# A four-layer graph network with two mixtures of experts: first tiles of the second mixture from the rows routed so far, and five reordered seams

## The chip, the cores and the metric

The kernel runs on one core of a Trainium2 chip. The metric is the device time of one execution in microseconds (us); the median of three runs stands for a kernel. One further execution was profiled, and the views quoted here come from it. The engines are TensorE (PE, its weight loads as PEld), VectorE (DVE), ScalarE (ACT), GpSimd (POOL) and SyncE (SP), which issues most of the transfers. Each engine works through its own list of instructions in order.

## The reference, cut to what matters

A graph of 2,708 nodes with 256 features each goes through four layers. Each is a graph convolution and then a feed-forward block, both with a layer norm in front and a residual. The change lies in layers 1 to 3:

```python
x = x + L1_gnn(layernorm(x), adj)        # graph attention, 4 heads of 64
x = x + L1_ffn(layernorm(x))             # first mixture: H = gelu(x @ W1 + b1), 1024 wide
    # assign = argmax(softmax(H @ Wg + bg)); y = H @ Wd[assign] + bd[assign]; out = prob * y
x = x + L2_gnn(layernorm(x), adj)        # graph attention, 1 head of 256
x = x + L2_ffn(layernorm(x)):            # decoder block
    # x = x + causal_attention(rmsnorm(x)) @ wo.T    4 heads, 2 shared keys and values
    # probs = softmax(rmsnorm(x) @ router.T); the two largest of 8, weights divided by their sum
    # out += weight[e] * ((silu(h @ w1[e].T) * (h @ w3[e].T)) @ w2[e].T)     682 wide
x = x + L3_gnn(layernorm(x), adj)        # graph attention, 1 head, elu
x = x + linear(layernorm(x))
```

## The kernel before

The nodes lie in 22 row tiles of 128 (the last has 20 rows) and in 6 blocks of 512 (the last has 148). `X` holds the features in SBUF throughout. A framework tracks tiles and buffers and places each engine's instructions in order by its own estimates, within the dependences; `tc.issue_after(i)` forbids an instruction of the same engine to be placed before `i`. A tile of a pool with `bufs=n` is reused after n others, when their last reader is done.

**`gat_heads`** (layer 1) takes two heads at a time, `p` = 0 and 1. For each of the 22 source tiles `j` the attention weights `e` are made, multiplied with `V` into six accumulators `acc` (L780) and with `low` into the denominators `den` (L788). After the last `j`, `den` is copied to `ds`, transposed, inverted to `rd`; then each of six accumulators is copied to `o`, transposed, multiplied by `rd` into `y` (L822) and added to `X` (L829).

**`top1_ffn`** (first mixture) takes layer-norm statistics (`ln_stats`: sums on DVE in groups of four tiles, a root on ACT, L147), then block after block: `features` (normalise, transpose), `hidden` (32 records of PE, L911, Gelu on ACT), `gate` (logits, first maximum, rank of each row in its expert, and its number scattered to `fnodes` in DRAM), and `store`, which transposes hidden rows and writes them to DRAM (`hr` L926, three buffers). The last two blocks are stored after the last gate. `route.finish` then turns the counts into a list of tiles: each expert owns one tile for certain, the others follow, 26 in all as a rule. The node numbers of each tile are loaded from `fnodes` (L1550, L1554) as a column, 128 pieces of 4 bytes per tile, converted (L980), and used to gather hidden rows (`fetch`, L990). Each tile is transposed (L1003), multiplied with the expert's `wd`, and scattered to DRAM.

**`decoder_ffn`** (layer 2). In `attention`, each of six blocks is attended over all source tiles up to it (scores L1736, exponents L1749, values L1755); sums of exponents go by DVE and, for every third `j`, by POOL (L1761), and end in `pd` (L1767). The generator `send` runs a block behind, beside the next block's attention: projection `wy`, residual, root-mean-square norm, router logits `pr`, then `route.chunk` (first and second choice, rank L1423, scatter of normalised rows `h` to `hs` in DRAM, L1444). `yield` is where attention goes on; `steps` sets the pace. The last block's `send` runs alone after attention, then `route.finish`.

**`experts`** runs 47 tiles as a rule. Tiles 0 to 7 are the first 128 rows of experts 0 to 7. A step of its loop holds: `fetch` (rows `f` from `hs`, L1543 or L1550, five buffers), `front` (transposes, L116, copy `ft` L1891), `hidden` (w1 and w3, L1909), `silu` (L1922), `gate` (L1926), `transposes` (`pt` L1933), `results` (`po` L1941, copy `y`, indirect scatter `send` L1573) and `place` (`route.where`, L1563 to L1567: the rows of `ys` that the tile's results go to, held in `to`, eight buffers). After the first tiles' gate come `shares` (softmax of the routing logits) and `Head` (weights of layer 3). `route.others` guards tiles beyond the usual number.

**The join.** `Routing.combine` loads both results of each row from `ys` in six blocks (L1594) over SP and ACT and adds them to `X` (L1604) block after block, with layer 3's statistics between. `reload_graph` brings the mask back from DRAM, and `mark_empty` (L2084, L2085) writes a row of it on ACT's queue.

Of the kernel before, what the change touches and what calls it, by code (L numbers as in the profile page):

```python
# [16 lines left out]
P = 128  # L17
# [660 lines left out]
def gat_heads(net):  # L678
# [8 lines left out]
    Q = len(cols) // 2  # L687
    with ExitStack() as ctx:
        big = ctx.enter_context(tc.tile_pool(name="g1big", bufs=1))
        V = big.tile([P, NT, H, DH], F32, name="V")  # L690
        ratio = big.tile([P, NT, H], F32, name="ratio")

        low = big.tile([P, NT, H, 2 * Q - 1], F32, name="low")
        big_p = big.tile([P, H, N], F32, name="big_p")
# [73 lines left out]
        for p in range(2):  # L768
# [3 lines left out]
            nc.tensor.matmul(den, zero, big_p[0:1, 0, :512], start=True, stop=False, skip_group_check=True)  # L772
            for j in range(NT):
                e = wide.tile([P, 2, N], F32, name="e")
                for k, h in enumerate(heads):
                    gat_pairs(net, e[:, k, :], j, 0, N, big_p[:, h, :], ratio[:, j, h : h + 1])
                for n, (i0, iw) in enumerate(cols):
                    for k, h in enumerate(heads):
                        half = slice(k * DH, (k + 1) * DH)
                        nc.tensor.matmul(  # L780
                            acc[n][half, :iw], V[:, j, h, :], e[:, k, i0 : i0 + iw], start=j == 0, stop=j == NT - 1
                        )
                for q in range(Q):
                    for k, h in enumerate(heads):
                        for half in range(2):
                            i0, iw = cols[half * Q + q]
                            g = (2 * k + half) * 32
                            nc.tensor.matmul(  # L788
# [6 lines left out]
                            )  # L795

            ds = small.tile([P, 512], F32, name="ds", bufs=1)
# [4 lines left out]
            rd = small.tile([P, 4, 4, Q], F32, name="rd", bufs=1)  # L802
# [4 lines left out]
            out = []  # L807
            for n, (i0, iw) in enumerate(cols):
                o = small.tile([P, 512], F32, name="o", bufs=3)
                (nc.vector.tensor_copy if n % 2 else nc.scalar.copy)(o[:, :iw], acc[n][:, :iw])  # L810
                pt = paux.tile([P, 4, P], F32, name="aux")
                its = tiles_of(i0, iw)
                for c, i in enumerate(its):
                    r = rows(i)
                    nc.tensor.transpose(pt[:r, c, :], o[:, c * P : c * P + r], net.ident)
                whole = [c for c, i in enumerate(its) if rows(i) == P]
                for c0, c1, r in [(0, len(whole), P)] + [(c, c + 1, rows(its[c])) for c in range(len(whole), len(its))]:
                    nt = c1 - c0
                    y = small.tile([P, 4, 2, DH], F32, name="y")

                    d = rd.rearrange("p c (k b) q -> p c k b q", b=2)[:r, c0:c1, :, n // Q, n % Q]
                    nc.vector.tensor_tensor(  # L822
                        y[:r, :nt],
                        pt[:r, c0:c1, :].rearrange("p c (k d) -> p c k d", d=DH),
                        d.unsqueeze(3).to_broadcast([r, nt, 2, DH]),
                        ALU.mult,
                    )
                    xs = X[:r, its[0] + c0 : its[0] + c1, p * 2 * DH : (p + 1) * 2 * DH]
                    nc.vector.tensor_tensor(xs, xs, y[:r, :nt].rearrange("p c k d -> p c (k d)"), ALU.add)  # L829
# [27 lines left out]
def top1_ffn(net, ctx):  # L857

    nc, tc, a, X = net.nc, net.tc, net.a, net.X
    E, HID = 8, 1024
    KC = HID // P
    with ExitStack() as inner:
        big = ctx.enter_context(tc.tile_pool(name="f1big", bufs=1))
        dram = ctx.enter_context(tc.tile_pool(name="f1dram", bufs=1, space=bass.MemoryType.DRAM))
        wd = inner.enter_context(tc.tile_pool(name="f1wd", bufs=1, side="right")).tile([P, E, KC, D], F32, name="wd")
# [11 lines left out]
        for e in range(E):  # L879
            nc.sync.dma_start(wd[:, e], a["f1_wd"][e].rearrange("(c p) m -> p c m", p=P))  # L880
        route = Routing(net, big, dram, 1, "f")
        ln = net.ln_stats()
# [3 lines left out]
        with tc.tile_pool(name="f1tp", bufs=2, space=PSUM) as ptp, tc.tile_pool(  # L886
# [7 lines left out]
            def features(its):  # L894
                ft = work.tile([P, 2, 512], F32, name="ft")
                for k, t in enumerate(its):
                    r = rows(t)
                    f = rp.tile([P, D], F32, name="f", bufs=2)
                    net.normed(f, t, ln)
                    ps = net.transposed(ptp, f, r)  # L900
                    nc.vector.tensor_copy(ft[:, :, k * P : k * P + r], ps[:, :, :r])
                return ft

# [14 lines left out]
            def store(its, halves):  # L918

                for k, t in enumerate(its):  # L920
                    r = rows(t)
                    for n, half in enumerate(halves):
                        hr = rp.tile([P, 512], F32, name="hr", bufs=3)
# [3 lines left out]
                        (nc.scalar.copy if n else nc.vector.tensor_copy)(  # L927
                            hr[:r], ps[:r].rearrange("p c m -> p (c m)")
                        )
                        nc.sync.dma_start(rows_of[span(t), n * 512 : (n + 1) * 512], hr[:r])  # L930
# [17 lines left out]

            blocks, kept = chunks(512), []
            ft = features(tiles_of(*blocks[0]))  # L950
            for n, (n0, nw) in enumerate(blocks):
                its = tiles_of(n0, nw)
                halves = hidden(ft, nw)
                if n + 1 < len(blocks):
                    ft = features(tiles_of(*blocks[n + 1]))
                gate(its, halves, nw)
                kept.append((its, halves))
                if n + 2 != len(blocks):
                    for k in kept:
                        store(*k)  # L960
                    kept.clear()
        route.finish()
        prep = ctx.enter_context(tc.tile_pool(name="g2prep", bufs=1))
        with tc.tile_pool(name="f1t", bufs=1, space=PSUM) as pt, tc.tile_pool(
# [3 lines left out]
            nc.scalar.dma_start(bd.rearrange("p e d -> p (e d)"), a["f1_bd"].rearrange("e d -> (e d)").partition_broadcast(P))  # L968

            node, number, to = (  # L970
                sp.tile([P, route.tiles], t, name=name, bufs=1)
                for t, name in ((F32, "node"), (I32, "number"), (I32, "to"))
            )
            usual = route.usual
            groups = [range(E)] + [range(s, min(s + 4, usual)) for s in range(E, usual, 4)]
            held = {}

            def numbers(group):
                g = slice(group[0], group[-1] + 1)
                nc.vector.tensor_copy(number[:, g], node[:, g])  # L980

            def places(group):
                g = slice(group[0], group[-1] + 1)
                at = sp.tile([P, E], F32, name="at", bufs=2)[:, : len(group)]
                nc.vector.tensor_tensor(at, node[:, g], route.taken[:, g], ALU.mult)
                nc.vector.tensor_tensor(to[:, g], at, route.spare[:, g], ALU.add)

            def fetch(s):
                hr = held[s] = sp.tile([P, 2, 4, P], F32, name="hr", bufs=5)
                nc.gpsimd.indirect_dma_start(  # L990
# [22 lines left out]
            route.load_first(node[:, :E])  # L1013
            for s in range(E, usual):
                route.load(s, node[:, s : s + 1])
            numbers(groups[0])
            for s in range(4):
                fetch(s)
            ready = transposes(0)
            route.owners()  # L1020
            places(groups[0])
# [3 lines left out]
            def through(s0, s1, ready):  # L1025
                last = added = None
                for s in range(s0, s1):
# [14 lines left out]
                    route.send(to[:, s : s + 1], y)  # L1042
                    with tc.issue_after(added.ins):
                        for g in groups[1:]:
                            if s + 6 == g[0]:
                                numbers(g)
                                places(g)
                        if s == 3:
                            heads.append(Head(net, prep, one, "g2", True, nc.scalar))
# [4 lines left out]
            with route.others():  # L1054
                group = range(usual, route.tiles)
                for s in group:
                    route.load(s, node[:, s : s + 1])
                numbers(group)
                places(group)
# [32 lines left out]
def gat_single(net, key, head, feed, elu):  # L1092
# [7 lines left out]
    with ExitStack() as ctx:  # L1100
# [6 lines left out]
        nc.gpsimd.memset(V[:, LAST], 0.0)  # L1107
# [1082 lines left out]
```

## Time and profile before

| what | value |
|---|---|
| time, median of 3 runs | 2879.4 us (2875.14 to 2881.12) |
| the profiled execution | 2876.56 us |
| its span | 2874.8 us |
| mean granted TensorE clock | 0.951 of full speed |
| PE busy | 2630.7 us, 92% |
| DVE busy | 1448.3 us, 50% |
| ACT busy | 1037.4 us, 36% |
| POOL busy | 369.4 us, 13% |

Times on the page are microseconds from the span's start. A timeline line reads: start, duration, engine, source line, operation, output and inputs, shapes, count; in brackets the idle time of the engine before it and what ended it. The rows of digits cut the span into 40 slices of 71.9 us: the busy share in tenths, and for PEclk the clock that TensorE was granted.

Where the stages lie, by PE: `gat_heads` up to 1068; first mixture's hidden 1093 to 1228, its experts 1245 to 1360; layer 2's convolution to 1645; decoder attention 1660 to 2125; second mixture's experts 2162 to 2552; layer 3's convolution 2577 to 2840.

### The profile page before, as it was taken

How to read it: one execution, taken by the hardware profiler on the slowest of the kernel's cores; microseconds unless marked ns; L12 is line 12 of the kernel's file. 1: busy time of each engine (PE TensorE's matmuls, PEld its weight loads, DVE VectorE, ACT ScalarE, POOL GpSimd, SP SyncE). 2: the span in 40 equal slices, each digit the busy share in tenths (PEclk: the TensorE clock that was granted, in tenths of full speed). 3: DMA queues.
4: the chain of work that ended last, by engine and by line, in shares of the span. 5: the costliest groups of instructions: out<-in, count | busy, mean ns of one | idle time of the engine just before them, and what ended most of it. 6: DMA issues, size and time to landing. Idle time of an engine off the chain costs nothing. (4 is left out here: it accounts for less than half of the span.)

```text
span 2874.8 us, 32363 instructions
## 1 busy us (share of the span) xinstructions
PE 2630.7 (92%) x11709; PEld 1604.0 (56%) x11709; DVE 1448.3 (50%) x3078; ACT 1037.4 (36%) x1636; POOL 369.4 (13%) x456
## 2 busy tenths in 40 slices
PE   5999989799999998979899899999969999969998
PEld 4667746563333334568688533333337777747885
DVE  7753358354777774432644456455653222235455
ACT  3344433224665653311543223233322222225453
POOL 0000012100000001133200023223331111110002
PEclk9999999698999998989999999899979999989999
DMA  8899210000000005253300100002031010041001
GB/s 296 290 301 327 81 65 1 8 1 1 1 1 1 1 17 176 82 173 108 114 1 0 34 22 17 15 0 93 15 116 32 30 34 30 30 147 49 1 1 39
DMA packets 113727, 197.67 MB, mean 69 GB/s; under 512 B 12380, under 2 KB 71636, under 8 KB 110732
## 3 DMA queue, kind: packets, MB, share of 16 engines
q1 hardware_dynamic: 92758, 147.89, 15.8%
q0 software_dynamic: 13120, 38.06, 4.1%
q10 hardware_dynamic: 7690, 9.62, 1.1%
q8 instruction: 98, 1.61, 0.2%
q14 instruction: 61, 0.50, 0.1%
HBM read 135.82 MB, written 59.71 MB: 68 GB/s over the span
## 5 line engine op out<-in xcount | busy, mean ns | idle before, releaser
L675 DVE SCALAR_TENSOR_TENSOR e<-e,mask 128x768 f32<-128x768 f32 (+2 forms) x264 | 411.5, 1573 | 311.0 <-ACT e L674 310.8
L674 ACT ACTIVATE e<-big_p,minus_one,ratio 128x768 f32<-128x768 f32 (+2 forms) x264 | 394.9, 1513 | 363.4 <-PE acc L1236 230.0
L1236 PE MATMUL acc<-V,e 128*128 128x257 f32 (+1 forms) x1936 | 433.5, 383 | 4.5 <-DVE e L675 4.4
L1236 PEld LDWEIGHTS acc<-V,e 128*128 128x128 f32 (+1 forms) x1936 | 352.4, 186 | 85.6 <-issue 32.1
L780 PE MATMUL acc<-e,V 128*64 128x512 f32 (+1 forms) x1056 | 249.7, 550 | 4.1 <-DVE e L675 4.1
L1909 PE MATMUL h<-w,ft 128*128 (+1 forms) x752 | 233.6, 453 | 0.5 <-ACT ft L1891 0.5
L284 PE MATMUL acc<-F,e 128*128 128x257 f32 x968 | 226.3, 384 | 2.9 <-DVE e L281 2.5
L284 PEld LDWEIGHTS acc<-F,e 128*128 128x128 f32 x968 | 173.5, 185 | 66.8 <-DVE e L281 28.1
L780 PEld LDWEIGHTS acc<-e,V 128*64 128x64 f32 x1056 | 95.4, 137 | 180.7 <-issue 159.1
L1736 PE MATMUL sc<-qt,kt 64*128 64x512 f32 (+5 forms) x568 | 176.6, 574 | 4.1 <-ACT e L1749 2.4
L1749 ACT ACTIVATE e<-sc 128x1024 f32<-128x1024 f32 (+3 forms) x120 | 99.6, 859 | 190.9 <-PE sc L1736 174.4
L1909 PEld LDWEIGHTS h<-w,ft 128*128 128x128 f32 x752 | 136.2, 191 | 56.7 <-issue 1.4
L281 DVE TENSOR_TENSOR e<-e,mask 128x512 f32<-128x512 f32 (+2 forms) x132 | 80.5, 625 | 150.4 <-ACT e L275 148.7
L1761 DVE TENSOR_TENSOR sum<-sum,e 128x1024 f32<-128x1024 f32 (+4 forms) x88 | 99.8, 1135 | 79.3 <-ACT e L1749 76.4
L275 ACT ACTIVATE e<-score 128x512 f32<-128x512 f32 (+2 forms) x132 | 69.7, 544 | 178.9 <-PE score L273 152.2
L1941 PE MATMUL po<-w,ht 114*128 (+1 forms) x564 | 129.5, 379 | 0.9 <-DVE ht L1934 0.9
L1755 PE MATMUL po<-e,V 128*64 128x512 f32 (+3 forms) x480 | 112.2, 549 | 16.8 <-ACT e L1749 8.7
L788 PE MATMUL den<-e,low 128*3 128x512 f32 (+1 forms) x1056 | 123.1, 542 | 0.0
L1941 PEld LDWEIGHTS po<-w,ht 114*128 114x128 f32 x564 | 106.7, 189 | 22.6 <-DVE ht L1934 8.2
L1563 DVE TENSOR_SCALAR second<-f,down 128x1 f32<-128x1 f32 x47 | 9.9, 212 | 213.0 <-DMA f<-hs 213.0
L273 PE MATMUL score<-QK 128*128 128x512 f32 (+2 forms) x264 | 112.1, 555 | 1.2 <-ACT e L275 0.7
L1736 PEld LDWEIGHTS sc<-qt,kt 64*128 64x128 f32 (+1 forms) x568 | 60.4, 189 | 92.5 <-issue 76.4
(606 smaller groups left out, 3496.3 us busy)
## 6 DMA issues: line engine op xcount, KB each, us to landing
row<-in_adj SPq DMA_DIRECT2D x21, 1354.0 KB
raw<-in_adjT SPq DMA_DIRECT2D x35, 768.0 KB
hs<-zero SPq DMA_DIRECT2D x8, 2838.0 KB
hidden<-hr SPq DMA_DIRECT2D x42, 256.0 KB
wd<-in_f_wd SPq DMA_DIRECT2D x8, 1024.0 KB
kept<-mask SPq DMA_DIRECT2D x21, 338.5 KB
mask<-kept SPq DMA_DIRECT2D x21, 338.5 KB
f<-hs SPq DMA_DIRECT2D x47, 129.0 KB
```

The costliest lines, as they stand in the source:

```text
L273: nc.tensor.matmul(ps[:r, :iw], QK[:, 0, span(j)], QK[:, 1, i0 : i0 + iw], start=True, stop=True)
L284: nc.tensor.matmul(acc[k][:ri], e[:r, k * P : k * P + ri], F[:r, j, :], start=j == 0, stop=j == NT - 1)
L674: nc.scalar.activation(v, big_p[:, i], AF.Relu, bias=net.minus_one, scale=ratio)
L675: return nc.vector.scalar_tensor_tensor(v, v, 1.0, net.mask[:, j, i], ALU.add, ALU.mult)
L780: nc.tensor.matmul(acc[n][half, :iw], V[:, j, h, :], e[:, k, i0 : i0 + iw], start=j == 0, stop=j == NT - 1)
L788: nc.tensor.matmul(den[g : g + Q, :iw], low[:, j, h, Q - 1 - q : 2 * Q - 1 - q], e[:, k, i0 : i0 + iw], start=False, stop=j == NT - 1 and ...
L1236: nc.tensor.matmul(acc[k][:ri], e[:, k * P : k * P + ri], V[:, j, :], start=j == 0, stop=j == NT - 1)
L1736: nc.tensor.matmul(by_pairs(ps[:r, g])[:, :, o:], kt[b, span(j)], qt[b, :, o:iw], start=True, stop=True)
L1755: nc.tensor.matmul(by_pairs(po[b])[:, :, o:], V[:r, j, g, :], by_pairs(e[:r, g])[:, :, o:], start=j == 0, stop=j == last,)
L1761: (nc.gpsimd if part else nc.vector).tensor_tensor(total, total, ev, ALU.add)
L1909: last = nc.tensor.matmul(halves[s, n][:, q, :HALF], fts[s][:, c, :], weights.w13[n][:, es[s], c, q * HALF : (q + 1) * HALF], start=c == 0 ...
L1941: last = nc.tensor.matmul(po, ht[:KP, k, :], w2[:KP, es[s], k, :], start=k == 0, stop=k == KC - 1)
```

## The change

**Layer 1's graph attention and the first mixture.** The last `j` makes `den` before the values. `o` gets six buffers of its own, and for `p` = 1 the six adds are handed over as a function `add`, which `top1_ffn` calls between its statistics; roots beyond block 0 are found by Newton steps on DVE. The `wd` loads move behind stores of blocks 0 to 3. The last two blocks are stored with all copies on ACT and eight spare buffers. Node numbers are loaded as rows of 512 bytes and transposed by PE; the `bd` load and layer 2's `Head` move from ACT's queue to POOL's.

```diff
+                for step in (values, weights) if j + 1 < NT else (weights, values):
+                    with tc.issue_after(last.ins):
+                        last = step(e, j)
...
+            turn(add, 0, ptp, "tp")
+            turn(stats.sums, *tiles[0])
+            turn(add, 1, ptp, "tp")
+            turn(stats.roots, *tiles[0])
             ft = features(tiles_of(*blocks[0]))
+            turn(stats.sums, *tiles[1], root=False)
+            turn(add, 2, ptp, "tp")
+            turn(stats.sums, *tiles[2], root=False)
+            turn(stats.newton, rp, tiles[1][0], tiles[2][1])
...
+                if n == 0:
+                    for m in range(3, len(blocks)):
+                        turn(add, m, ptp, "tp")
+                        turn(stats.sums, *tiles[m], root=False)
+                    turn(stats.newton, rp, tiles[3][0], NT)
...
+                    stored = store(*kept.pop())
+                    with tc.issue_after(stored.ins):
+                        for e in range(2 * n, 2 * n + 2):
+                            nc.sync.dma_start(wd[:, e], a["f1_wd"][e].rearrange("(c p) m -> p c m", p=P))
...
-                        (nc.scalar.copy if n else nc.vector.tensor_copy)(
+                        (nc.scalar.copy if n or late else nc.vector.tensor_copy)(
...
+                ps = pt.tile([P, len(group)], F32, name="node", bufs=1)
+                nc.tensor.transpose(ps, rowed[here, :], net.ident[here, here])
+                nc.vector.tensor_copy(number[:, g], ps)
...
-            f, self.hs.rearrange("(e c) d -> c (e d)", e=self.E)[:P, :]
+            f, self.hs.rearrange("(e c) d -> e (c d)", e=self.E)[:, :P]
```

**The second mixture.** The last block's `send` is no longer run after attention. `route.cut` counts the rows of blocks 0 to 4 and keeps the first eight tiles' destinations by that count. `experts` starts at once: `through` loads all eight first tiles, three over ACT's queue and five over POOL's, and calls `step()` at several places of its loop; each call runs the generator `routing` one yield further (the last block's `send`, `route.finish`, `route.owners`, and the `Head` of layer 3), with its PSUM tiles in the one buffer that `front` uses. What is left of it runs out at `s == 4`. `shares` moves behind the last tile. If an expert had fewer than 128 rows at the cut and got more, `further` becomes so large that the guarded branch runs, which now does tiles 0 to 7 again first. `f` gets eight buffers. In the last block's attention POOL takes no sum in the last four `j`, and block 4's `send` is paced at 24 instead of 14.

```diff
-                part = j % 3 == 2
+                part = j % 3 == 2 and (m == 1 or j + 4 < last)
...
+                steps[1] += 14 if n + 1 < len(cols) else 24
...
+        route.cut(aux, "aux")
         core.close()
         weights.more()
-        for _ in send(len(cols) - 1):
-            pass
+        mixture(exp, lambda *work: send(len(cols) - 1, *work))
...
+            fs[s] = work.tile([P, D + 2], F32, name="f", bufs=E)
+            route.load(s, fs[s], engine)
...
+            def step():
+                with tc.issue_after(last.ins):
+                    next(beside, None)
+
+            for s in range(s0, min(s0 + (E if cut else 4), s1)):
+                fetch(s, (nc.scalar if s < 3 else nc.gpsimd) if cut else None)
...
             silu(s0)
+            step()
...
             gate(s0)
-            if s0 == 0:
-                route.owners()
-            place(s0)
-            place(s0 + 1)
-            if s0 == 0:
-                shares()
+            step()
+            place(s0, cut)
+            place(s0 + 1, cut)
...
                 silu(s + 1)
+                step()
                 with tc.issue_after(last.ins):
                     last = results(s, ht)
-                if s + 4 < s1:
+                step()
+                if s == 4:
+                    for _ in beside:
+                        pass
+                if s + 4 < s1 and (s + 4 >= E or not cut):
                     fetch(s + 4)
...
+        def routing():
+            pool = ctx.enter_context(ExitStack())
+            yield from rest(pool.enter_context(tc.tile_pool(name="e_r", bufs=1)), pf, "tp")
+            route.finish(pf, "tp")
+            yield
+            route.owners()
...
+            with tc.issue_after(gates[-1].ins):
+                head(room)
...
+        through(0, route.usual, routing(), True)
+
+        with tc.issue_after(gates[-1].ins):
+            shares(rooms[0])
         with route.others():
+            through(0, E)
             through(route.usual, route.tiles)
```

The functions that are new in `Routing`:

```diff
+    def cut(self, psum, tag):
+        nc.tensor.matmul(ps, self.net.ones, self.count, start=True, stop=True)
+        self.had = pool.tile([P, E], F32, name=f"{key}had")
+        nc.vector.tensor_scalar(self.had, ps, float(P), None, ALU.min)
+        own, taken, spare = self.cuts = [pool.tile([P, E], F32, name=f"{key}cut{k}") for k in range(3)]
...
+        if self.cuts:
...
+            nc.vector.scalar_tensor_tensor(
+                self.further, missing[:, :1], float(S), sums[:1, 3, 4 + E - 1 :], ALU.mult, ALU.add
+            )
```

**The join.** The results are loaded over SP and POOL; of ACT's queue one load is left, that of block 0's second results. The mask's empty row moves to POOL's queue, and POOL's part of `reload_graph` is placed behind the last of its reads. In `gat_single` the memsets of `V` and `ratio` move to DVE, and a Sqrt activation on one column is added at the start.

```diff
+        queues = nc.sync, nc.gpsimd
...
-                    (nc.sync, nc.scalar)[(n + c) % 2].dma_start(
+                    engine = nc.scalar if n == 0 and c else queues[(n + c) % 2]
...
-        reload_graph(net, kept)
+        with net.tc.issue_after(route.read.ins):
+            reload_graph(net, kept)
...
+        nc.scalar.activation(small.tile([P, 1], F32, name="warm", bufs=1), net.ln_eps, AF.Sqrt)
```

## The prediction

> **What bounds the kernel now.** I read the page's busy rows first, then the timeline at each hole of the PE row, then the waits.
>
> ```profile
> PE 2630.7 (92%) x11709; PEld 1604.0 (56%) x11709; DVE 1448.3 (50%) x3078; ACT 1037.4 (36%) x1636; POOL 369.4 (13%) x456
> PE   5999989799999998979899899999969999969998
> PEclk9999999698999998989999999899979999989999
> ```
>
> TensorE is busy 92% of the span: 244 us are idle, and only idle or half-clocked time can be won, since the diff leaves the matmuls of experts and attention as they are. Slices 15 to 17, 29 to 30 and 35 to 36 (71.9 us each) hold the seams that the diff touches. The timeline of the first mixture:
>
> ```profile
> 1068.31 0.69 DVE L798 COPY ds<-den 128x512 f32<-128x512 f32 x1 [4.85 <-PE den L788]
> ...
> 1082.29 0.30 ACT L147 ACTIVATE sd<-mv,ln_eps 128x4 f32<-128x4 f32 x1 [7.25 <-DVE mv L145]
> ...
> 1226.95 1.03 PE L926 MATMUL hr<-ident,ht 128*20 128x128 f32 x4 [1.08 <-ACT hr L927]
> ...
> 1231.44 0.41 SPq L1554 DMA_DIRECT2D node<-fnodes  x1
> ...
> 1238.78 0.17 DVE L980 CAST number<-node 128x8 int32<-128x8 f32 x1 [6.26 <-DMA node<-fnodes]
> ...
> 1245.11 1.94 PE L1003 MATMUL ht<-ident,hr 128*128 128x128 f32 x8 [17.14 <-issue]
> ```
>
> The bracket is the idle time before a line and what ended it. The first root comes 14 us after the last denominators, the first hidden matmul at 1093.36. Later the node numbers take 7.3 us from issue to use. The timeline where attention ends and the second mixture's experts begin:
>
> ```profile
> 2124.17 1.25 PE L1767 MATMUL pd<-sum,ones 128*64 128x296 f32 x4 [3.75 <-POOL sum L1761]
> ...
> 2150.79 0.66 PE L116 MATMUL tp<-ident,f 128*128 128x128 f32 x2 [9.23 <-DMA f<-hs]
> ...
> 2161.65 0.87 PE L1933 MATMUL pt<-ident,hh 128*114 128x128 f32 x6 [1.21 <-DVE hh L1926]
> ```
>
> PE waits for POOL's sum, then for the last block's routing: 36 us from the last `pd` to the first `pt`. Inside the experts, the timeline and the waits view:
>
> ```profile
> 2217.49 0.21 DVE L1563 TENSOR_SCALAR second<-f,down 128x1 f32<-128x1 f32 x1 [5.30 <-DMA f<-hs]
> 2218.13 0.87 DVE L1926 TENSOR_TENSOR hh<-hh,h 128x682 f32<-128x682 f32 x1
> 2219.05 0.87 PE L1933 MATMUL pt<-ident,hh 128*114 128x128 f32 x6 [0.18 <-DVE hh L1926]
> ```
>
> ```profile
> DVE second L1563 <- DMA f<-hs: 213.0, 41, 5.5
> ```
>
> `second` (a tile's destination) stands in DVE's queue ahead of the gate. Most of the 213 us cost nothing, but in the chain of waits the steps are 8.15 us up to 2211 and then 8.48 (35 steps from 2211.47 to 2508.20), with the load of `f` and the gate in them. Last, the timeline of the join:
>
> ```profile
> 2562.37 3.26 DVE L1604 SCALAR_TENSOR_TENSOR X<-y,dweight,X 128x256 f32<-128x256 f32 x8 [6.58 <-DMA y<-dys]
> ...
> 2576.41 0.30 ACT L147 ACTIVATE sd<-mv,ln_eps 128x4 f32<-128x4 f32 x1
> 2577.52 1.73 PE L1134 MATMUL tp<-ident,f 128*128 128x128 f32 x7 [25.12 <-DVE f L108]
> ```
>
> `mv` is ready at 2567.4; ACT is held by its own queue's loads, the empty mask row (2572.51, 2574.33) and a 1.28 us table load.
>
> **Part 1, the first mixture's start: −11.5.** Today all six adds of the second pass precede the first root. After: add 0, statistics of block 0, add 1, root. From the last den T=1068.2: `rd` stands at T+2.9 as now; transposes and y and X of .66, .69, .68, four statistics of .56 (2.2), add 1 of 1.4, root and reciprocal .5, four normalised tiles with copies 3.2: first hidden at about T+12, 1080, against 1093.4. The four adds left (1.4 each), five blocks of statistics (2.2) and two Newton roots (2.3) are about 21 us of DVE; they are covered by hidden(0) and hidden(1), 14 to 17 us of PE each. If the cover fails, block 1's features come late by up to 5. Gain 8 to 15; of the 13, 11.5 taken. The `wd` loads (8 of 1 MB) go on SP behind stores of blocks 0 to 3; those stores end long before the experts at 1230, so nothing waits for them. Values after denominators at the last j of the first pass: in the 35 us where pass 0 gives way to pass 1 PE is busy throughout; 0 (−1 to +2).
>
> **Part 2, its stores and node numbers: −15.** Stores end at 1228 because three `hr` buffers wait for landings (waits of 7.3 us on ACT, 3.3 on PE). With 8 spare buffers and all 12 copies on ACT at 0.58, paced by transposes of about 1, the last lands at 1224. Numbers as rows of 512 B instead of 1,024 pieces of 4 B: 2 us for the load (as `f<-hs` shows), .6 for PE transpose and cast, 5.2 to the first gathered rows as now less the `bd` load moved behind: experts at about 1230. `bd` and the next layer's weights go to POOL's queue: 0.3 to 1.0 each behind four fetches; `fetch(4)` is 8 us away. Bounds −8 (stores still bound by landings) to −18.
>
> **Part 3, attention to experts: −18.** The sum leaves POOL: −4, pd ends at 2121.2. The first tiles hold rows of blocks 0 to 4, all scattered by then, so loads of `f` and w3 issue at 2121.4; `f` lands at 2124, tile 0 needs tp, copy and 16 hidden records at half clock (8.5 as now), gate .9: first `pt` at 2134 instead of 2161.65, −27.5. Back come: last block's PE work wy, tp, pr, rank, total in the steps, 3.7 at full clock; its DVE work, some 60 small ops of .17 to .47 plus owners, 25 us, spread over the 40 us of five steps that carry 2.2 us of DVE each, but ahead of gates at times; and one PSUM buffer shared with the tile transposes, together +5; the faster pacing of block 4 inside attention +1. Net −18, bounds −28 (all hidden) and −3 (each piece stalls a step by 4). What else the step issues: four scatters on POOL (.97 each, 1.3 apart), ahead of which only sends stand, needed in the join; SP's loads of tiles 8 on, which wait for the row numbers of the full count. Those are written when the routing ends, in step 4 at the latest, about 2170; tile 8 is transposed at 2183, so 13 us cover a load of 2.0. If the routing slipped to step 7, PE would stand still for each us beyond that. The next layer's attention weights, now on ACT, feed DVE products that waited 2.84 for `av`; behind those stand gates, so one step can lose up to 5, inside the bounds. `cut` adds one matmul and five small ops (1 us of DVE in attention's idle tail), the redo test four more; the table of Silu is loaded earlier, where ACT waits for nothing: 0, as its 1.28 lay in front of hidden's end before. The shares of the mixture leave for the end of the experts: about 3 us of DVE, hidden until `y` lands 9 us after the last `po`.
>
> Five of the first loads go over POOL, three over ACT. The Trainium skill ("DMA: Bandwidth & Descriptors", Specifications and Issuing engine by pattern) speaks against that: a gpsimd load has its first byte after about 1 us against 0.6, and simple loads belong to sync. The trace: `f<-hs` from SP lands in 2.0 us, POOL's `g3w` in 3.8 and `av` in 5.1, with others of theirs beside. By the rule tile 3 is late by 0.4 us, by the row by up to 3; it is needed 24 us later, so both make 0 of it. For the join, see part 5.
>
> **Part 4, `f` buffers 5 to 8: −8.** A load is now freed by a transpose in the very step in which its `second` stands ahead of the gate. With 8 it is issued three steps sooner. But `to` has 8 buffers too: `to` of tile j is free when the send of tile j−8 has landed. That send issues at 2166.95 and lands 2.4 later, 2169.35; the gate starts at 2168.89. If the scheduler puts the gate first, 35 × .33 = −11.5. If it puts the place first, the gate starts .75 late in 39 steps, +29. No view of before shows which; I lean to the gate first, since it is ready first, and take −8 (−11.5 to +29).
>
> **Part 5, the join: −5.5.** With ACT's queue left one y load and no mask row, and Sqrt not needed behind them, root at 2568, first `tp` at 2571 behind add 1 instead of 2577.5: 6.3. POOL's y loads come later by 0.4 (rule) to 2 (rows); only blocks 1 on need them, and DVE spends 3.3 per block: −3 to −7. The mask row, its memset (2.35) and the 22 mask loads now stand behind POOL's last read, about 6 us later than before; they ended by 2594 and are first used after 2620, so 20 us cover that. The memsets of V and ratio (.31, .10) on DVE come while it waits for `y`: 0.
>
> A second rule ("TensorE: Matmul & The Clock Gate", What's actually happening): after 3.4 us idle the array runs at half clock for the next 3.4 busy ones. The trace's first 8 hidden records take 6.22 us, .78 each, later ones .44. By the rule holes of 10 us still pay their warm-up, 1.7 each, so I credit none; if shortened holes kept the clock, 3 × 1.7 = 5 more.
>
> **Sum.** −11.5 −15 −18 −8 −5.5 = −58. The profiled execution took 2876.56 (span 2874.8): 2818.6. The median of the runs, 2879.4, is 2.8 higher: 2821.
>
> **Rivals.** (a) The stall stays or part of the small gains are lost: −8 becomes +1 to +3, 2830 to 2832. For: 41 waits on `f` exist already. (b) Routing is not really beside: shared PSUM and DVE order give back 15, 2836. This is also the case that the change doesn't do what it says. For: PE waits .2 to 1.2 for the gate already. Redoing eight tiles (8 × 8.15 = 65) needs an expert with fewer than 128 rows in the first 2,560; the reference's routing on its inputs gives 485 at least, so I leave it out. (c) Places wait for sends ahead of the gate at 2.4 us: −11.5 −15 −18 −5.5 −11.5 + 29 = −32, 2847. (d) Slower: the same wait with longer landings. Every us of landing adds one to each of 39 steps; −61.5 + 39 × (.75 + L − 2.4) is zero at L = 3.2 us. The last two sends, with others beside, took 3.3; at 3.6 the time is 2894. Against: the median of 47 sends is 2.4.
>
> **How the numbers follow.** As forecast .62, own range 2803 to 2836; (a) .14; (b) .11; (c) .09; (d) .04. All best ends and the clock's 5 together are −84.5, 2795 on the median's scale; 5 above (c) is the upper end. Range 2795 to 2852, which leaves out (d) and the outer part of (c). The runs spread 0.2%, which is about what can be told from no change: faster .95, same .01, slower .04.
>
> **What would show it.** Right: first hidden by 1082; experts' first `ht` 26 us earlier than before; no POOL in front of `pd`; first `pt` 12 to 15 us behind it; no stall of 0.18 in front of `pt` and steps of 8.15; root within 2 us of `mv`. Wrong: steps above 8.5 with DVE's `to` waiting for `dys`; PE waiting for `tp` or gates in the first five steps; first `hidden` still behind DVE; extra `h` records showing a redo.

## The result, and the profile after

| kernel | median | runs | ratio to before, 95% interval |
|---|---|---|---|
| before | 2879.6 us | 4, 2875.1 to 2881.1 | |
| after | 2855.1 us | 4, 2849.2 to 2856.4 | 0.9913 [0.9896, 0.9931] |

The kernel became faster by 24.5 us, where 58 were forecast; 2855 lies above the range. The profiled execution of after took 2849.18 us (span 2847.5), the fastest of its four, against 2876.56 before. Between these two, 27.4 us have to be explained.

The page's busy rows, as shown of before:

```profile
PE 2621.5 (92%) x11714; PEld 1617.1 (57%) x11714; DVE 1450.7 (51%) x3097; ACT 1041.5 (37%) x1641; POOL 379.4 (13%) x471
PE   6999989799999999888999899998988999969998
PEclk9999999798999999989999999899989999989999
```

In the slice that holds the end of attention (the thirtieth, counted from the left) the 6 of before has become an 8, but the next one, in the experts' first steps, has gone from 9 to 8: what the seam gained was partly given back later. The timeline of the first mixture:

```profile
1056.77 0.69 DVE L836 COPY ds<-den 128x512 f32<-128x512 f32 x1 [2.85 <-PE den L816]
...
1066.83 0.30 ACT L147 ACTIVATE sd<-mv,ln_eps 128x4 f32<-128x4 f32 x1 [1.36 <-DVE mv L145]
...
1072.45 4.47 PE L943 MATMUL h<-ft,w 128*128 128x512 f32 x8
...
1213.04 0.32 SPq L1658 DMA_DIRECT2D rowed<-fnodes  x1
1214.98 0.17 DVE L1050 CAST number<-node 128x8 int32<-128x8 f32 x1 [0.43 <-PE node L1049]
...
1220.19 1.97 PE L1074 MATMUL ht<-ident,hr 128*128 128x128 f32 x8 [5.24 <-DMA hr<-hidden,number]
...
1249.12 0.43 DVE L657 TENSOR_TENSOR a1t<-g2w,av 128x256 f32<-128x256 f32 x1 [6.58 <-DMA av<-in_g_a]
...
1254.04 5.41 PE L1110 MATMUL y<-wd,ht 128*128 128x256 f32 x16 [3.20 <-DVE g2grow L1161]
```

The first hidden matmul comes 11 us behind the end of `gat_heads` instead of 25, and the node numbers take 1.9 us from issue to use instead of 7.3. The last two lines are new: DVE waits 6.6 us for `av` of the next layer's `Head`, and PE stands 3.2 us behind DVE. Where attention ends and the second mixture's experts begin:

```profile
2092.11 1.45 POOL L1875 TENSOR_TENSOR sum<-sum,e 128x592 f32<-128x592 f32 x1
2093.59 0.66 ACT L1863 ACTIVATE e<-sc 128x592 f32<-128x592 f32 x1 [4.59 <-POOL sum L1875]
2094.31 1.25 PE L1869 MATMUL po<-e,V 128*64 128x296 f32 x4 [3.84 <-ACT e L1863]
...
2106.03 2.24 PE L1881 MATMUL pd<-sum,ones 128*64 128x296 f32 x8
2120.68 0.82 PE L2052 MATMUL pt<-ident,hh 128*114 128x128 f32 x6
...
2151.86 0.43 DVE L657 TENSOR_TENSOR a1t<-g3w,av 128x256 f32<-128x256 f32 x1 [1.19 <-DMA av<-in_g_a]
...
2154.64 5.31 PE L2060 MATMUL po<-w,ht 114*128 114x256 f32 x12 [5.67 <-DVE ht L2053]
```

From the end of `pd` to the first `pt` there are 12.4 us instead of 36.2, and `pd` no longer waits for POOL's sum; but 12 us ahead of it ACT and then PE now do. Inside the experts, the timeline of one step and the waits view of this stage (us in total, times, longest):

```profile
2319.41 0.21 DVE L1668 TENSOR_SCALAR second<-f,down 128x1 f32<-128x1 f32 x1 [5.33 <-DMA f<-hs]
...
2320.22 0.16 DVE L1672 TENSOR_TENSOR to<-second,dspare 128x1 int32<-128x1 f32 x1 [0.29 <-DMA dys<-y,to]
2320.30 0.87 DVE L2045 TENSOR_TENSOR hh<-hh,h 128x682 f32<-128x682 f32 x1
2321.22 0.87 PE L2052 MATMUL pt<-ident,hh 128*114 128x128 f32 x6 [0.47 <-DVE hh L2045]
...
2329.97 0.87 PE L2052 MATMUL pt<-ident,hh 128*114 128x128 f32 x6 [0.47 <-DVE hh L2045]
```

```profile
DVE second L1668 <- DMA f<-hs: 179.0, 33, 6.0
DVE to L1672 <- DMA dys<-y,to: 19.4, 27, 6.2
```

The step is 8.75 us (2321.22 to 2329.97); 8.74 is the usual length. `second`, `to` and then the gate `hh` still stand in this order in DVE's queue, and `to` now waits for the landing of a send. Last, the join:

```profile
2541.77 3.25 DVE L1715 SCALAR_TENSOR_TENSOR X<-y,dweight,X 128x256 f32<-128x256 f32 x8 [6.00 <-DMA y<-dys]
2546.81 0.30 ACT L147 ACTIVATE sd<-mv,ln_eps 128x4 f32<-128x4 f32 x1 [11.33 <-DVE mv L145]
2550.60 1.73 PE L1208 MATMUL tp<-ident,f 128*128 128x128 f32 x7 [18.36 <-DVE f L108]
```

The root now waits for `mv` and not for its own queue's loads. The balance by stages, cut at PE's first or last record of each in the two profiled executions:

| part | stages | forecast | measured |
|---|---|---|---|
| 1 | attention of layer 1: 371.1 to 365.4 (−5.7); to the first hidden: 25.1 to 11.0 (−14.1); hidden: 120.2 to 124.2 (+4.0); everything ahead of it (−1.1) | −11.5 | −16.9 |
| 2 | total of the counts to the first `ht`: 31.6 to 23.5 (−8.1); experts: 114.8 to 120.9 (+6.1) | −15 | −2.0 |
| 3 | decoder attention: 455.8 to 459.2 (+3.4); `pd` to `pt`: 36.2 to 12.4 (−23.8); first four steps: 32.6 to 42.8 (+10.2) | −18 | −10.2 |
| 4 | the other steps: 353.6 to 364.2 | −8 | +10.6 |
| 5 | last `pt` to layer 3: 29.7 to 22.9 | −5.5 | −6.8 |
| else | layer 2's convolution, layer 3 | 0 | −2.2 |
| sum | | −58 | −27.5 |

### The profile page after: what moved, and what is told of

Its sections match the earlier page's. It is cut to its first block, busy times and chain, and to the rows that moved or that the text cites. A ratio compares the mean times of both kernels' runs of the same rounds, so it can differ in the third digit from the quotient of the medians.

```text
span 2847.5 us, 32395 instructions
## 1 busy us (share of the span) xinstructions
PE 2621.5 (92%) x11714; PEld 1617.1 (57%) x11714; DVE 1450.7 (51%) x3097; ACT 1041.5 (37%) x1641; POOL 379.4 (13%) x471
## 5 line engine op out<-in xcount | busy, mean ns | idle before, releaser
L805 PE MATMUL acc<-e,V 128*64 128x512 f32 (+1 forms) x1056 | 242.7, 548 | 4.4 <-DVE e L675 4.4
L805 PEld LDWEIGHTS acc<-e,V 128*64 128x64 f32 x1056 | 107.8, 137 | 161.9 <-issue 129.2
```

The lines of the kernel that those rows point to most:

```text
L805: made = nc.tensor.matmul(acc[n][half, :iw], V[:, j, h, :], e[:, k, i0 : i0 + iw], start=j == 0, stop=j == NT - 1)
```

## The experiments

Ratios are to before, run on the same chip.

**Which buffer holds the steps?** The theory was that `to` alone does: with eight `f` and sixteen `to` the steps should be 8.15.

```diff
-        to = work.tile([P, 1], I32, name="to", bufs=8)
+        to = work.tile([P, 1], I32, name="to", bufs=16)
```

> The changed kernel with 16 instead of 8 buffers for `to`, nothing else. Theory: in the changed kernel the step of the experts is 8.74 us because the write of `to` (L1672) waits in DVE's queue, ahead of the gate, for the landing of the send of eight tiles before; with 16 buffers it waits for nothing, the step falls to 8.15, some 34 steps x .59 = 20 us less, about 2828 profiled, and `dys<-y,to` leaves the chain. Rival: the wait on `f` (L1668), which also stands ahead of the gate, takes its place, the step stays at 8.5 as before the change: 6 to 8 us less at most, or nothing if the step is set by the loads themselves.

2845.5 us, 0.988 [0.9861, 0.99]; from the first to the last `pt` 396.2 us instead of 407.0. The steps fell to 8.45, not to 8.15. Its waits view and its timeline:

```profile
DVE second L1668 <- DMA f<-hs: 175.1, 34, 5.8
```

```profile
2233.29 0.21 DVE L1668 TENSOR_SCALAR second<-f,down 128x1 f32<-128x1 f32 x1 [5.24 <-DMA f<-hs]
2233.92 0.86 DVE L2045 TENSOR_TENSOR hh<-hh,h 128x682 f32<-128x682 f32 x1
```

The `dys` wait is gone and the gate still starts .63 behind `second`. The rival came true: the wait on `f` takes its place, and the step is about what it was before the change.

**The edit of `f` alone in the kernel before** takes it out of its surroundings.

```diff
-            fs[s] = work.tile([P, D + 2], F32, name="f", bufs=5)
+            fs[s] = work.tile([P, D + 2], F32, name="f", bufs=8)
```

> The kernel before with 8 instead of 5 buffers for `f`, nothing else of the change. Theory: loading rows three steps sooner moves the place of a tile so far ahead that it runs into the send of eight tiles before: the step goes from 8.48 to 8.74, 9 to 10 us slower than before. Rival (what the prediction leaned to): the gate goes first and the stall of .33 in 35 steps is gone, 8 to 11 us faster.

2891.5 us, 1.0048 [1.0036, 1.006]: slower. From the first to the last `pt` 403.0 us against 386.2. Its waits in the experts and its timeline:

```profile
DVE second L1563 <- DMA f<-hs: 200.0, 37, 5.6
...
DVE to L1567 <- DMA dys<-y,to: 28.0, 33, 6.2
```

```profile
2306.49 0.16 DVE L1567 TENSOR_TENSOR to<-second,dspare 128x1 int32<-128x1 f32 x1 [0.33 <-DMA dys<-y,to]
...
2307.49 0.87 PE L1933 MATMUL pt<-ident,hh 128*114 128x128 f32 x6 [0.47 <-DVE hh L1926]
```

So this line of the diff costs 13 us of the whole, 17 in this stage, by itself, through the wait that case (c) named.

**Both buffers in the kernel before.**

```diff
+        to = work.tile([P, 1], I32, name="to", bufs=16)
+            fs[s] = work.tile([P, D + 2], F32, name="f", bufs=8)
```

> The kernel before with 8 buffers for `f` and 16 for `to`. Theory: neither the load nor the landing is then late, steps of 8.15 throughout, 10 to 12 us faster than before. Rival: the stall belongs to the order of DVE's queue and stays with whatever `second` waits for: within 3 us of before.

2878.4 us, 0.9989 [0.998, 0.9999], 386.0 us from first to last `pt`: the same as five and eight buffers. The waits view of the whole run still has the line:

```profile
DVE second L1563 <- DMA f<-hs: 197.9, 38, 5.6
```

With five buffers or eight, `second` is placed in the step in which its buffer has just been loaded again. That left the order in DVE's queue as the theory. It can be tested by stating the order.

**The place behind the gate.** The gate's last instruction of each step is kept, and the place of tile `s + 2` may not be put ahead of the latest one.

```diff
+            gated.append(nc.vector.tensor_tensor(h2, h2, halves.pop((s, 1))[:, :, :HALF], ALU.mult))
...
+                    with tc.issue_after(gated[-1].ins):
                         place(s + 2, ...)
```

In after:

> The changed kernel with the place of tile s+2 ordered behind the gate of tile s on VectorE; buffers stay 8 and 8. Theory: with any number of buffers VectorE's order puts a place into the step in which its buffer is set free, ahead of a gate, so it always waits for a transfer just issued (f: 8.45, `to`: 8.74). Kept behind a gate two tiles earlier it finds both long landed: steps of 8.15, first to last `pt` from 407.0 to about 386, 20 us less. Rival: a place late in the step holds the load or the send of its own tile back, and the step stays at 8.4 or more.

2831.5 us, 0.9849 [0.982, 0.9878]; from first to last `pt` 385.9 us, 21.1 fewer than after. Its timeline:

```profile
2236.23 0.87 DVE L2045 TENSOR_TENSOR hh<-hh,h 128x682 f32<-128x682 f32 x1 [5.64 <-PE h L2028]
2237.01 0.21 DVE L1668 TENSOR_SCALAR second<-f,down 128x1 f32<-128x1 f32 x1
2237.15 0.87 PE L2052 MATMUL pt<-ident,hh 128*114 128x128 f32 x6
```

The gate waits for `h` alone, `second` finds its rows there, `pt` has no bracket, and the step is 8.16. In before:

> The kernel before with that same ordering alone and none of the change. Theory: its steps fall from 8.48 to 8.15 too, first to last `pt` from 386.2 to about 375, 11 us faster than before. Rival: with five buffers for `f` the place is what sets a load free, so a later place makes a later load, and the transposes wait: same or slower.

2865.5 us, 0.996 [0.995, 0.9971]; 375.3 against 386.2, steps of 8.15 to 8.16. Buffers, loads and sends are the same as without the edit, so the order explains the stall in both kernels, with five buffers or eight. In before it was worth 10.9 us in the stage; in after, where it grew, 21.1.

**The moved `Head`s.** Layer 2's goes back to ACT's queue, and layer 3's gets an `av` of its own.

```diff
-    heads.append(Head(net, prep, one, "g2", True))
+    heads.append(Head(net, prep, one, "g2", True, nc.scalar))
...
-        av = net.load_rows(work, a[f"{key}_a"], 2 * D, "av", engine=engine)
+        av = net.load_rows(own or work, a[f"{key}_a"], 2 * D, "av", engine=engine)
```

> The changed kernel with layer 3's `av` in a buffer of its own (in the changed kernel it reuses the room of the last block's routing and waits for its scatters to land) and layer 2's `Head` loaded over ACT's queue as before the change. Theory: the steps of tiles 3 and 4 lose no 7.8 us to DVE products that wait for `av` (2151.84), and the first mixture's experts no 5.6 at 1250: the first falls to at most 3, the second to at most 1; 10 to 13 us less in all. Rival: the stall of tiles 3 and 4 is DVE's own backlog of small routing operations, and the one of the first mixture is the `bd` load behind four fetches on POOL: then less than 3 us change.

2853.7 us, 0.9911 [0.9893, 0.9929]: as after in total, where 10 to 13 us were expected. By stage, the first mixture's experts took 116.3 us against 120.9, so POOL's queue cost 4.6 of the 6.1 there. The step of the second mixture's tile 3 took 15.14 against 15.92: the shared buffer of `av` was not what held it. Its join took 26.4 against 22.9, with the last `po` at half clock, 5.46 us against 2.83, which gives most of the gain back.

**Spare buffers and the last sums.** The stores' second group gets four buffers out of `w1`, and POOL leaves the sums of the last seven `j` instead of four.

```diff
-            for k in kept:
-                store(*k, True, room)
-                room = ()
+            more = [w1[:, c, h * 512 : (h + 1) * 512] for c in range(2) for h in range(2)]
+            for k, own in zip(kept, (room, more)):
+                store(*k, True, own)
...
-                part = j % 3 == 2 and (m == 1 or j + 4 < last)
+                part = j % 3 == 2 and (m == 1 or j + 7 < last)
```

> The changed kernel with two edits in stages that lie far apart. The last two blocks' stores get four more spare buffers (from `w1`, which is done by then), so that all twelve copies have one: theory, the last copy waited 4.4 us for a landing and SP's row of node numbers stood behind it, so the stretch from the total of the counts to the first gathered tile falls from 23.5 to about 19; rival, SP is busy with the expert weights and the stretch stays. And POOL's last sum in the last block's attention (it stood behind eight scatters that the faster pace had put there, and ScalarE and TensorE waited for it) goes to VectorE: theory, attention falls from 459.2 to about 456, first to last `pd`; rival, the scatters delay nothing else and VectorE's extra sum costs as much: same.

2849.9 us, 0.9902 [0.9877, 0.9926]. From the total to the first `ht` it took 22.0 us against 23.5, not 19: buffers bound little of it. Attention was 451.3 against 459.2, more than the 3.84 us of the wait in after; all of this gain lies in the last block. With that wait gone the records behind it run at full clock, 0.72 us where after had 1.25. Its timeline, which has `pd` 5.4 earlier:

```profile
2099.50 0.72 PE L1869 MATMUL po<-e,V 128*64 128x296 f32 x4 [1.53 <-DVE e L1867]
...
2100.65 2.09 PE L1881 MATMUL pd<-sum,ones 128*64 128x296 f32 x8
```

Only 5 of these 9.4 us are left in the total. In the experts, which neither edit touches, it took 413.0 from the first to the last `pt` instead of 407.0, with 26.1 us of waits of `to` for `dys` instead of 19.4, and the join took 25.7 instead of 22.9.

**The routing not beside.** First all of the last block's routing, then the first tile.

```diff
+            for _ in beside:
+                pass
+            with tc.issue_after(route.totaled.ins) if cut else nullcontext():
+                front(s0)
...
-            with tc.issue_after(gates[-1].ins):
-                head(room)
+            head(room)
```

> The changed kernel with the whole routing of the last block ahead of the first tile, as before the change, all other parts kept. Theory: the stretch from the last `pd` to the first `pt` goes back from 12.4 to about 30, and the first four steps fall from 42.8 to 33: about 8 us slower than the changed kernel, which is what running the routing beside the tiles is worth net. Rival (the prediction's sum): it is worth 15 or more. Second rival: since the stall of tile 3 gives most of it back, it is worth nothing.

2863.1 us, 0.993 [0.9909, 0.9952]: 8 us slower than after (7 than the next run, on the same chip). `pd` to `pt` is 27.7 instead of 12.4, the first steps 10.3 and then 8.16, and first to last `pt` 398.7 instead of 407.0. The core of the change thus brings 15 us at the seam and gives 8 back in the steps, 7 net.

**The queues of the first loads.** All eight over SP.

```diff
-                fetch(s, (nc.scalar if s < 3 else nc.gpsimd) if cut else None)
+                fetch(s)
```

> The changed kernel with all eight first loads of `f` on SP's queue instead of three on ACT's and five on POOL's. Theory: SP issues them ahead of the w3 loads, each .33 apart, so the first hidden matmul comes 2 us later and nothing else changes: 2 us slower. Rival[...]: the loads come earlier, `second` of the first tiles waits less, 1 to 2 us faster.

2855.7 us, 0.9902 [0.9883, 0.9922], and 12.4 from `pd` to `pt` as in after. Which queue they take makes no difference, as the prediction has it; the 2 us of the expectation did not come.

**What was found, together.** After with the place behind the gate, the buffers and sums of the run above, layer 2's `Head` over ACT and layer 3's made after the last tile's gate.

```diff
-            with tc.issue_after(gates[-1].ins):
-                head(room)
...
+            with tc.issue_after(gated[-1].ins):
+                head(rooms[0])
```

> The changed kernel with everything together: places behind gates, spare buffers for all stores, POOL's last sum on VectorE, layer 2's `Head` over ACT's queue, layer 3's `Head` behind the last gate instead of in the routing's last step. Theory: 21 + 4.5 + 3 + 4.6 us as the single edits, and the step of tile 3 falls from 15.9 to about 12.5 since eight VectorE products leave it: 36 us less than the changed kernel, about 2819. Rival: the step of tile 3 is bound by the routing's own chain of small operations and does not fall, and the late `Head` comes back at the join: about 2825 or more.

2818.7 us, 0.9805 [0.9785, 0.9825]. The step of tile 3 took 9.5 us instead of 15.9, so most of its stall was the `Head` on DVE (the other edits leave it: the step took 15.9 with the place alone behind the gate, 16.3 with the buffers and sums, 15.1 with `av` in its own buffer). Its timeline, where after had a wait of 5.67:

```profile
2143.86 2.86 PE L2060 MATMUL po<-w,ht 114*128 114x256 f32 x12 [1.71 <-DVE ht L2053]
```

But from the total to `ht` it took 26.3: on ACT's queue the `Head`'s loads stood before the last copies of the stores. The next run moves them to SP and gives the node numbers' row tile the place of `wg`, whose last reader is done.

```diff
-            rowed = sp.tile([P, P], F32, name="rowed", bufs=1)
+            rowed = wg.rearrange("p c m -> p (c m)")[:, :P]
...
-    heads.append(Head(net, prep, one, "g2", True, nc.scalar))
+    heads.append(Head(net, prep, one, "g2", True, nc.sync))
```

> The version with everything together, and two edits more: the row of node numbers lands in `wg`, which is done by then, instead of a new tile in the room of the stores' buffers, and layer 2's `Head` loads go over SP's queue instead of ACT's. Theory: SP's row load waited for the stores' landings because its tile reuses their room, not because a copy was late (four more spare buffers moved it only from 23.5 to 22.0); now it goes once the scatters have landed and only the gather of `hidden` rows waits for the stores, so the stretch from total to first gathered tile falls from 26.3 to about 20, 2813. Rival: the stores' landings bound the gather as well, and the stretch stays at 22 or more; only what ACT's queue lost (3 to 4) comes back.

2801.1 us, 0.9735 [0.9712, 0.9758], the fastest version of the study. From the total to `ht` it took 21.5 and not 20; its waits view in this stretch says why:

```profile
SPq L1658 <- DMA fnodes<-ftag,fto: 2.0, 1, 2.0
```

The row load waits for the scatter of the numbers to land. Another 10.7 us came where nothing had been aimed at: attention took 440.4 against 451.1. One stretch of it, first of the version before, with everything together, and then of this one (columns: stretch, length, busy us and count of PE, PEld, DVE, ACT, POOL, granted clock, DMA share, GB/s):

```profile
1829.00:1889.00 60.00, 57.25 (x188) 19.31 (x188) 28.21 (x34) 17.47 (x26) 16.71 (x11) 0.89 0.00 0
```

```profile
1827.00:1887.00 60.00, 56.54 (x208) 19.50 (x208) 34.94 (x50) 18.76 (x29) 16.70 (x11) 1.00 0.00 0
```

PE is equally busy in both, at a clock of 0.89 and of 1.00. In the first of the two PE worked from 1825.4 to 1842.5 without a break at a granted clock of 0.50, and at 0.51 from 1938.0 to 1944.9; in this version the same instructions had 1.00 in both places. These 24 us at half clock are 12 at full clock, which is about the 10.7. So this part of the gain came by the clock and is no merit of the two edits, as far as the runs show; without it the version would lie at about 2812 (an estimate, 2801.1 and 10.7).

## Why the prediction was wrong

The direction and the places were right, the sum was not: 27.5 came of 58. The 30.5 missing are 18.6 in part 4, 13.0 in part 2, 7.8 in part 3, less 5.4 in part 1, 1.3 in part 5 and 2.2 elsewhere.

**Part 4 is the step that failed.** "I lean to the gate first, since it is ready first" chose between −11.5 and +29 and took −8. The place stood first, as case (c) had it, with steps of 8.74 where that case's price gives 8.90 (8.15 and .75). The reason given does not hold: readiness in the trace is no evidence of the order in DVE's queue, which is fixed before. Before already showed that order: `second` ahead of the gate, with a wait of 5.3, in the lines that the prediction quoted, and between the two the line of `to` (the third here). The first two lines are from one of the first six steps, where `to` stood behind the gate: `second` waits as long, and the step is 8.16.

```profile
2201.13 0.21 DVE L1563 TENSOR_SCALAR second<-f,down 128x1 f32<-128x1 f32 x1 [5.25 <-DMA f<-hs]
2201.52 0.87 DVE L1926 TENSOR_TENSOR hh<-hh,h 128x682 f32<-128x682 f32 x1 [0.17 <-PE h L1909]
...
2218.05 0.16 DVE L1567 TENSOR_TENSOR to<-second,dspare 128x1 int32<-128x1 f32 x1
```

The assumption behind −8, that an earlier load frees the gate, fell with the third experiment: sixteen and eight buffers gave the steps of eight and five. Only the stated order gave 8.16, and it was worth 10.9 us in before: the good case was priced rightly at 11.5, but its cause was the order and not the buffers.

**Part 2 was mis-sized by two terms.** The numbers as rows did what they should (7.3 to 1.9). The stores did not end at 1224 with an early row load: the load of the row, not the buffers, was last. Four more buffers gained 1.5, and with the row tile freed the load waited for the scatters. The gain was 8.1 instead of 15; 8 was the lower bound given. The second term was not in the sum: `Head` and `bd` on POOL's queue were followed to the next `fetch` there, and not to DVE, whose products wait for `av`, nor to what is queued behind them. The stage grew by 6.1, of which 4.6 came back with the `Head` on ACT's queue; the other 1.5 are not explained by a run.

**Part 3 held at the seam and failed in attention.** The first `pt` came 23.8 us sooner behind `pd`. The prediction's −27.5 holds the 4 by which `pd` itself was to end sooner, so it has 23.5 for the same stretch. Of what was to come back, 8.7 without the pacing, the four steps took 10.2, but not as it was told, a little in each: for the greater part it is a single step, tile 3's 15.9, with the `Head`'s products of DVE in it. "One step can lose up to 5" lay at 7.8 and was in no sum; that the total nearly fits is luck. What fails is the first term. That POOL leaves the last sums was to gain 4, and the pacing to cost 1; attention became 3.4 longer, and these 6.4 us are most of the 7.8. The wait in front of `pd` did go, and another one came: eight scatters of block 4 stood on POOL ahead of its last sum (2081.9 to 2091.1 in the trace), the exponent waited for that sum's buffer, and PE stood 3.84 and then ran at half clock to the end. That the faster pacing put the scatters there is argued from the code; no run took the pacing back. With the sums off POOL early enough (the run with spare buffers) attention was 451.3, 4.5 less than before: the forecast 4 were there to be had.

**Part 1 was better than forecast.** "PE is busy throughout; 0" for the loop was wrong by 5.7: the busy row, 9 in every slice there, cannot show what PE loses. The trace puts 4.7 of the 5.7 where the first pass of heads gives way to the second: the last accumulator was copied out 18.5 us behind the first pass's last record before, and 3.1 after. That the six `o` buffers are the reason fits this; no run took them away. The phase of hidden matmuls grew by 4.0: 1.4 are transposes that moved into it, and 2.6 are a wait of PE at 1121.5 behind DVE, whose copy of `hr` waited 3.6 for a store to land. The `wd` loads now stand between these stores, where the prediction had nothing waiting; whether they are the reason was not tried.

**Part 5 was right**: −6.8 for −5.5, with the root waiting for `mv` as it should. Of the rivals (c), at 2847, came nearest, and its mechanism is the one that the runs showed, with 10.6 lost in part 4 where (c)'s terms make 17.5. The routing beside the steps, which (b) doubts, is worth 7 net.

## What to carry to other kernels

Where an instruction that waits for a transfer stands ahead of the critical one in an engine's queue, state the order; more buffers only change what it waits for, and can make it worse. When a load is moved to another queue, follow it to the products that wait for it and to what is queued behind these, not only along the queue. A choice between two signs of one term, here −11.5 and +29, is to be settled by the order seen in the trace of before, not by which of two is ready first.

## What the runs showed of the hardware

A short wait of PE can cost more than its length. The 3.84 us wait at the end of attention was followed by records of 1.25 us that take 0.72 without it, and the stage became 8 us shorter when it went. The granted clock was 0.50 from 2091.4 to 2108.4, the end of the stage, though PE worked without a break from 2094.3 to 2103.0; in the run without the wait it was 0.92 over the last 14 us. Before has the same at its wait of 3.75: the four `pd` behind it take 1.25, the four ahead of it 0.72. The prediction credited nothing for the clock, by the rule that it takes from the Trainium skill ("TensorE: Matmul & The Clock Gate", What's actually happening): half clock for the next 3.4 busy us. These traces differ from it. Here half clock lasted 8.7 us of unbroken work, and 17.1 in attention of the version with everything together, so the price of 1.7 that the prediction made of the rule is too low for these waits.

Half clock also came without such a wait. The last `po` took 5.46 us at a granted 0.50 with the moved `Head`s, and 2.83 at 1.00 in after, behind the same waits of 1.42 and 0.88 in both; in four of the runs it took 4.4 to 5.5, and the join some 3 us more. The fastest version had three runs at 2799.8 to 2801.1 us with a mean clock of 0.965 or 0.966, and two of 2810.0 and 2813.9 with 0.961, so some 10 of its us go with the clock. What decides it stays open; between kernels whose instructions in attention are nearly the same, slight differences in the order of DVE's sums are all that the traces show.

Open too is what bounds the stretch from the total of the counts to the first `ht`, which took 21.5 to 26.3 us in the versions with the change: in the fastest one SP was released at 1213.7, 8.7 us after the last scatter's issue (1205.04), and no run took the scatters away.
